# Another split of SBUF homes, earlier unpacking, earlier state sums and two more identity products in a linear-attention and GeGLU kernel

## The chip, the cores and the metric

The kernel runs on one core of a Trainium2 chip. The metric is the device time of one execution in microseconds; where several runs were made, their median.

## What is computed

The input x is 4 sequences of 512 tokens by 512 channels, in float32. Two residual layers follow each other:

```python
x = x + _L0_attn_ref(_layernorm(x, axis=-1), ...)
x = x + _L0_ffn_ref(_layernorm(x, axis=-1), ...)
```

The first is a gated linear attention with 4 heads of 128, in chunks of 128 tokens (4 chunks per sequence). q, k and v are linear in the normalized x; k is normalized per head; alpha is a sigmoid and beta a softplus of two small linear maps. Within a chunk, scores q k^T are weighted with beta and with a causal decay from the running sum of log(alpha), and multiply v. Across chunks a 128 x 128 state per head is carried: a chunk's result takes q times the state before it, and

```python
new_state = state * td_i + d_i      # d_i = v^T (k * beta * decay to the chunk's end)
```

The second is a GeGLU network with 4096 hidden units. Its three weight matrices come as 4-bit codes with a scale per 32 inputs and are unpacked on the chip:

```python
gelu = jnp.tanh(0.7978845608028654 * (gate + 0.044715 * gate ** 3)) * gate * 0.5 + gate * 0.5
inter = gelu * up
out = jnp.einsum('tn,hn->th', inter, Wd)
```

## The kernel before

All instructions stand in an order written out by hand; each engine runs its own in that order, and semaphores make it wait for others.

**Attention.** For each sequence b there are 12 steps: four products for v (`product_v`, psum tiles pva and pvb), four for q (pq) and four for k (pk, added to its bias by VectorE at L428). A step has a number p, and `behind(p)` issues what goes behind its product. Chunk work runs some steps behind: for each chunk, at p % 3 = 0, the transposed k (tpk, kT) and the decay weights dm (pc, exponentials on ScalarE, a mask on GpSimd, and from chunk 1 on q times the decay, qc, on GpSimd); at p % 3 = 1, the scores sp, multiplied into dm by VectorE (L606); at p % 3 = 2, `chunk_sums`: the state's addition dp (L617), the chunk's result yp (L626, L628), and behind them VectorE's addition of yp to the residual tile xr (L637), whose result SP stores to accd (L638), the state's update on VectorE (L646, L651 or, for the last sequence, four operations at L655), and the second layer norm (`second_norm`). That norm's tile is transposed one step later (tp_f) and split in three parts g (L366 on ScalarE, L367 and L368 on VectorE), which SP stores to DRAM (h, L370).

**MLP.** A product of float32 values is made of three parts of 12 bits each ("hi", "lo", "mi"), so each weight block has three rounded tiles. The 32 gate/up blocks are worked on in 35 rounds, four blocks at a time for one sequence of 512 tokens per round, the sequences in turn. A round holds 12 x tiles, loaded from h (L300). For each block, `gate_up` makes two products (pa with 8 matrix instructions, pb with 4, L777); ScalarE and VectorE make the result t of them (L782, L783), a gelu (L789), the product of gate and up (L794), and its three parts i (L797, L801, L802). `down` multiplies these with the down weights (p_d, L821), adds the sums to four tiles acc (L829, L833) and SP stores these (L836). A product of 512 columns by a 128 x 128 weight is one matrix instruction here. The first MLP rounds (one, two and three blocks) run between the chunk steps of the last sequence: round 0 between its k products, round 1 and 2 with its last chunks.

**Unpacking.** A block of weights is unpacked in six steps: fields (L179), masked (L184), scaled (L188), hi (ScalarE, L194), lo (L197) and mi (L200). `unpack(slots, upto)` issues the next step where it is called: behind two of three attention steps from the second sequence on, and behind MLP products. `more` takes the next fetched block when three large homes are free, and `fetch` issues the six transfers of a gate/up block or the two of a down block.

**Homes.** SBUF is kept in two lists of homes: large ones ([P, 2, T], 4 KB per partition) for weights, q and the transposed x, and small ones ([P, T], 2 KB) for all else. `get` takes the home that has been free longest; `put` gives it back at once when the last reader has been issued, so that the next owner's first writer waits, by semaphores, for those readers and for a DMA that still reads the home. Where no small home is free, half of a large one is taken. PSUM has eight banks for tiles of one kind, which go round in the same way.

**Start.** Eight products of the identity (tile busy, L930) keep TensorE at work until the first normalized tile is there.

Of the kernel before, what the change touches and what calls it, by code (L numbers as in the profile page):

```python
# [14 lines left out]
ALU = mybir.AluOpType  # L15
# [6 lines left out]
P = 128  # L22
# [13 lines left out]
def f32(t):  # L36
    return t.bitcast(F32)
# [3 lines left out]
def tile_gated_linear_attention__then__nvfp4_geglu(  # L41
# [19 lines left out]
    nc = tc.nc  # L61
    B, T, D = x.shape
# [54 lines left out]
                else:  # L117
                    self.free.append(tag)

    two_k = Homes("a", 24, [P, 2, T])  # L120
    one_k = Homes("b", 42, [P, T], two_k)

    def psum(name):
        return fps.tile([P, T], F32, tag="p", name=name)
# [124 lines left out]
    loaded = []  # L249
    queue = []  # L250
    rounding = []

    def fetch():
        if waiting:
# [2 lines left out]

    def more():

        if not loaded or len(two_k.free) < 3:  # L260
            return
        nxt, start = loaded.pop(0)
        fields, masked, scaled, hi, lo, mi = start()

        def third():
            scaled()
            rounding.append(hi)

        def fourth():
            while rounding:  # L270
                rounding.pop(0)()
            lo()
            fetch()

        queue.insert(max(len(queue) - 2, 0), (0, fields))
        queue.extend([(0, masked), (nxt, third), (nxt, fourth), (nxt, mi)])
# [315 lines left out]
    def chunk_scores(b, n):  # L592
        toks = slice(n * P, (n + 1) * P)
        sp = psum(f"sp_{b}_{n}")
        kT = ch.pop("kT")
        for h in range(H):
            nc.tensor.matmul(  # L597
                sp[:, h * P : (h + 1) * P], f32(kT)[:, h * P : (h + 1) * P],
                f32(q_sb[b][h // 2])[:, h % 2, toks], start=True, stop=True,
            )  # L600
        one_k.put(kT)
        one_k.put(k_sb.pop((b, n)))
        if n == NCH - 1:
            two_k.put(*q_sb[b])
        dm = ch["dm"]
        nc.vector.tensor_tensor(f32(dm), sp, f32(dm), ALU.mult)  # L606

    def chunk_sums(b, n):
        v = v_sb.pop((b, n))
        old = state.get(b)  # L610
        if n + 1 < NCH:

            kw, new = ch.pop("kw"), ch.pop("new")
            dp = psum(f"dp_{b}_{n}")
            for h in range(H):
                hs = slice(h * P, (h + 1) * P)
                nc.tensor.matmul(dp[:, hs], f32(kw)[:, hs], f32(v)[:, hs], start=True, stop=True)  # L617
            state[b] = new
            one_k.put(kw)
        one_k.put(v)  # L620
        dm, vb = ch.pop("dm"), ch.pop("vb")
        qc = ch.pop("qc", None)
        yp = psum(f"yp_{b}_{n}")
        for h in range(H):
            hs = slice(h * P, (h + 1) * P)
            nc.tensor.matmul(yp[:, hs], f32(dm)[:, hs], f32(vb)[:, hs], start=True, stop=(n == 0))  # L626
            if n > 0:
                nc.tensor.matmul(yp[:, hs], f32(qc)[:, hs], f32(old)[:, hs], start=False, stop=True)  # L628
        one_k.put(dm, vb)
        if n > 0:  # L630
            one_k.put(qc)
            if b < B - 1 or n + 1 == NCH:
                one_k.put(old)
        a = acc.pop((b, n))

        def sums():
            nc.vector.tensor_tensor(f32(a), f32(a), yp, ALU.add)  # L637
            nc.sync.dma_start(accd[b * NCH + n], f32(a))  # L638

        def rest():  # L640
            if n + 1 < NCH:
                chunk_values(b, n + 1)
            if b < B - 1:
                second_norm(b, n, a)
            if n == 0:
                nc.vector.tensor_copy(f32(new), dp)  # L646
            elif n + 1 == NCH:
                pass
            elif b < B - 1:
                nc.vector.tensor_tensor(f32(new), f32(new), dp, ALU.add)  # L650
            else:  # L651

                for h in range(H):
                    hs = slice(h * P, (h + 1) * P)
                    nc.vector.scalar_tensor_tensor(  # L655
                        f32(new)[:, hs], f32(old)[:, hs], td[b][:, n * H + h : n * H + h + 1],
                        dp[:, hs], ALU.mult, ALU.add,
                    )
                one_k.put(old)
            if b == B - 1:  # L660
                second_norm(b, n, a)

        return sums, rest

# [252 lines left out]
    with tc.manual_schedule():  # L917
        wab_sb = const.tile([P, KC, 2 * H], F32, tag="wab", name="wab_sb")
        bq_sb = const.tile([P, H], F32, tag="bq", name="bq_sb")
        bab_sb = const.tile([P, 2 * H], F32, tag="bab", name="bab_sb")  # L920
        bv_sb, bk_sb = one_k.get("bv"), one_k.get("bk")
        wva = [two_k.get(f"wva{c}") for c in range(KC // 2)]
        wvb = two_k.get("wvb")
        wvb_ = f32(wvb).rearrange("p two (k n) -> p (two k) n", n=VB + 2 * H)
        wq, wk = ([two_k.get(f"w{nm}{c}") for c in range(KC // 2)] for nm in "qk")
        x0 = [load(tile_of(n), f"x0_{n}") for n in range(2)]

        busy = psum("busy")
        for i in range(8):
            nc.tensor.matmul(busy[:, :P], ident, ident, start=True, stop=True)  # L930

        warm = small.tile([P, 1], F32, tag="warm", name="warm")
        nc.scalar.activation(warm, eps_la, AF.Exp)
        for c in range(KC // 2):
            nc.sync.dma_start(f32(wva[c])[:, :, :VA], rows(Wv, c)[:, :, :VA])
        nc.sync.dma_start(
            wab_sb.rearrange("p (c two) n -> p c two n", two=2),
            Wab.rearrange("(c p two) n -> p c two n", p=P, two=2),
        )
        nc.sync.dma_start(f32(bv_sb), bv.partition_broadcast(P))  # L940
        for c in range(KC // 2):
            nc.sync.dma_start(wvb_[:, 2 * c : 2 * c + 2, :VB], rows(Wv, c)[:, :, VA:])
        nc.sync.dma_start(bab_sb, bab.partition_broadcast(P))
        x0 += [load(tile_of(n), f"x0_{n}") for n in range(2, NCH)]
        nc.sync.dma_start(bq_sb, bqT)
        for w, src in ((wq, Wq), (wk, Wk)):
            for c in range(KC // 2):
                nc.sync.dma_start(f32(w[c]), rows(src, c))
        nc.sync.dma_start(f32(bk_sb), bk.partition_broadcast(P))
        for n in range(NCH):  # L950
            xs[1, n] = load(tile_of(NCH + n), f"x1_{n}")

        def first(n):
            first_norm(0, n, x0[n])
            settle()

        for n in range(2):
            first_norm(0, n, x0[n])
        settle()
        nc.gpsimd.tensor_copy(wvb_[:, :, VB:], wab_sb)  # L960
        constants()
        turn("a", 1)
        blocks = mlp()
        p = 0
        for b in range(B):
            for j in range(3 * NCH):
                later = None
                if j < NCH:
                    if b == 0:

                        def between():
                            turn("a", 1)
                            if j + 2 < NCH:
                                first(j + 2)

                        product_v(b, j, between if j + 1 < NCH else None)
                    else:
                        product_v(b, j)
                elif j < 2 * NCH:
                    product_q(b, j - NCH)  # L980
                else:
                    later = product_k(b, j - 2 * NCH)
                if b == B - 1:
                    if j == NCH - 1:
                        two_k.put(*wva, wvb)
                        one_k.put(bv_sb)
                    elif j == 2 * NCH - 1:
                        two_k.put(*wq)
                    elif j == 3 * NCH - 1:
                        two_k.put(*wk)  # L990
                        one_k.put(bk_sb)
                if j == 3 * NCH - 1:
                    two_k.put(*hT[b])
                behind(p)
                if later:
                    later()
                if p in (5, 7):
                    fetch()
                if p > 3 * NCH and p % 3:
                    unpack(1, MT)  # L1000
                p += 1
                if b == B - 1 and j == 2 * NCH - 3:
                    load_x(0, jk)
                if b == B - 1 and j == 2 * NCH + 1:
                    for _ in range(2):
                        next(blocks)
                        behind(p)
                        p += 1
        for _ in blocks:
            behind(p)  # L1010
            p += 1


# [46 lines left out]
```

## Time and profile before

| | |
|---|---|
| median of 3 runs | 1312.18 us (1310.87 to 1312.48) |
| profiled execution, its own time | 1310.72 us |
| its span, first to last instruction | 1309.0 us |
| TensorE busy | 1298.8 us, 99% |
| VectorE busy | 955.3 us, 73% |
| ScalarE busy | 459.5 us, 35% |
| GpSimd busy | 122.6 us, 9% |
| DMA | 236.58 MB, mean 181 GB/s |

Times in the profile are those of one execution. Rows of TensorE are overlapped: one starts before the one ahead of it has left the array, so the time of a run of equal instructions is read from start to start. "Idle before" is the time in which an engine had nothing to run, and the releaser is the instruction whose semaphore ended it. SPq is the queue in which SP issues transfers in order.

### The profile page before, as it was taken

To read this page: it belongs to the slowest core of one execution; us is meant where nothing else is said; L and a number is where in the kernel's file an instruction comes from. 1 tells how busy PE (TensorE), PEld (TensorE's weight loads), DVE (VectorE), ACT (ScalarE), POOL (GpSimd) and SP (SyncE) were. 2 spreads that over 40 slices of the span, in tenths; PEclk is the share of its full clock that TensorE was granted. 3 is DMA by queue.
4 is the path that set the end of the run, shared out by engine and by line. 5 is a ranking of instruction groups with operands and counts; after the bars stand their busy time and mean duration, and the time that the engine had idled before them with its cause. 6 is when DMAs were issued, how large, how long until landed. Compare 5 with 4: busy or idle time off the path is not lost.

```text
span 1309.0 us, 17051 instructions
## 1 busy us (share of the span) xinstructions
PE 1298.8 (99%) x5822; PEld 1042.1 (80%) x5822; DVE 955.3 (73%) x1523; ACT 459.5 (35%) x906; POOL 122.6 (9%) x215
## 2 busy tenths in 40 slices
PE   9999999999999999999999999999999999999998
PEld 6677676778888888888888888888888888887886
DVE  3466666788767777777777777777777777777566
ACT  1443334753333333333333333333333333332332
POOL 1546363510000000000000000000000000000000
PEclk9999999999999999999999999999999999999999
DMA  7034436788555565656555555555555555555463
GB/s 242 9 97 132 120 104 201 237 263 276 189 174 196 176 195 176 193 175 195 181 190 182 189 183 187 184 187 183 187 185 186 180 190 186 184 178 194 167 247 132
DMA packets 173943, 236.58 MB, mean 181 GB/s; under 512 B 15776, under 2 KB 74400, under 8 KB 173856
## 3 DMA queue, kind: packets, MB, share of 16 engines
q1 hardware_dynamic: 173856, 235.49, 55.5%
q8 instruction: 46, 0.75, 0.2%
q14 instruction: 41, 0.34, 0.1%
HBM read 183.00 MB, written 52.43 MB: 180 GB/s over the span
## 4 chain that ended last, share of the span: by engine, by line
PE 96%; DMA 2%; DVE 1%; ACT 0%; issue 0%; POOL 0%; SPq 0%; DVEq 0%; ACTq 0%; POOLq 0%
PE pa L777 35%; PE p_d L821 26%; PE pb L777 17%; PE pk L422 4%; PE pq L410 4%; PE pva L385 2%; PE pvb L392 2%; DMA x<-h 1%; PE sp L597 1%; PE yp L626 1%; PE yp L628 1%; PE dp L617 1%; PE tp_a L345 1%; PE tp_f L345 1%; PE tpk L530 0%; PE pc L540 0%
## 5 line engine op out<-in xcount | busy, mean ns | idle before, releaser
L777 PE MATMUL pa<-x,wgu 128*128 128x512 f32 x2048 | 506.7, 389 | 0.0
L777 PEld LDWEIGHTS pa<-x,wgu 128*128 128x128 f32 x2048 | 383.9, 188 | 79.5
L821 PE MATMUL p_d<-wd,i 128*128 128x512 f32 x1542 | 356.5, 389 | 2.2 <-DVE state L655 1.1
L821 PEld LDWEIGHTS p_d<-wd,i 128*128 128x128 f32 x1542 | 288.3, 188 | 64.8 <-DVE i L801 1.6
L782 ACT ACTIVATE t<-pb 128x512 f32<-128x512 f32 x256 | 151.3, 591 | 359.8 <-PE pb L777 356.5
L777 PE MATMUL pb<-x,wgu 128*128 128x512 f32 x1024 | 274.8, 389 | 0.8 <-DMA x<-h 0.5
L783 DVE TENSOR_TENSOR t<-pa,t 128x512 f32<-128x512 f32 x256 | 176.5, 689 | 83.5 <-ACT t L782 78.1
L777 PEld LDWEIGHTS pb<-x,wgu 128*128 128x128 f32 x1024 | 192.2, 188 | 42.1 <-DMA x<-h 2.3
L829 DVE SCALAR_TENSOR_TENSOR acc<-p_d,acc 128x512 f32<-128x512 f32 (+1 forms) x137 | 93.3, 682 | 124.0 <-PE p_d L821 124.0
L797 ACT ACTIVATE i<-t 128x512 fp32r<-128x512 f32 x128 | 81.1, 633 | 192.4 <-DVE t L794 189.4
L789 ACT ACTIVATE t<-t 128x512 f32<-128x512 f32 x128 | 81.1, 633 | 135.5 <-DVE t L783 135.4
L801 DVE TENSOR_TENSOR i<-t,i 128x512 fp32r<-128x512 f32 x128 | 88.7, 693 | 23.6 <-ACT i L797 21.8
L833 DVE TENSOR_TENSOR acc<-acc,p_d 128x512 f32<-128x512 f32 x135 | 92.9, 688 | 14.1
L852 POOL TENSOR_TENSOR acc<-acc,last 128x512 f32<-128x512 f32 x1 | 1.3, 1289 | 1015.0 <-ACT last L851 1015.0
L794 DVE SCALAR_TENSOR_TENSOR t<-t,t 128x512 f32<-128x512 f32 x128 | 88.6, 692 | 4.3
L802 DVE SCALAR_TENSOR_TENSOR i<-i,t 128x512 fp32r<-128x512 f32 x128 | 88.1, 689 | 0.0
L422 PE MATMUL pk<-wk,hT 128*128 128x512 f32 x128 | 57.4, 592 | 0.0
L410 PE MATMUL pq<-hT,wq 128*128 128x512 f32 x128 | 57.4, 592 | 0.0
L410 PEld LDWEIGHTS pq<-hT,wq 128*128 128x128 f32 x128 | 23.7, 190 | 23.7 <-issue 23.2
L422 PEld LDWEIGHTS pk<-wk,hT 128*128 128x128 f32 x128 | 23.5, 190 | 23.6 <-issue 23.4
L200 DVE TENSOR_TENSOR wgu<-wgu,wgu 128x1024 fp32r<-128x1024 f32 x32 | 39.0, 1218 | 0.0
L197 DVE SCALAR_TENSOR_TENSOR wgu<-wgu,w_gu 128x1024 fp32r<-128x1024 f32 x32 | 38.9, 1216 | 0.0
(127 smaller groups left out, 941.5 us busy)
## 6 DMA issues: line engine op xcount, KB each, us to landing
x<-h SPq DMA_DIRECT2D x420, 256.0 KB
acc<-acc SPq DMA_DIRECT2D x256, 256.0 KB
h<-g SPq DMA_DIRECT2D x48, 256.0 KB
x<-in_x SPq DMA_DIRECT2D x16, 256.0 KB
pk_gu<-in_gate_p SPq DMA_DIRECT2D x32, 128.0 KB
sc_gu<-in_gate_s SPq DMA_DIRECT2D x64, 64.0 KB
pk_gu<-in_up_p SPq DMA_DIRECT2D x32, 128.0 KB
sc_gu<-in_up_s SPq DMA_DIRECT2D x64, 64.0 KB
```

The source lines that it names most:

```text
L410: nc.tensor.matmul(pq, f32(wq[k // 2])[:, k % 2, h * P : (h + 1) * P], f32(hT[b][k // 2])[:, k % 2, :], start=(k == 0), stop=(k == KC - 1),)
L422: nc.tensor.matmul(pk, f32(hT[b][k // 2])[:, k % 2, n * P : (n + 1) * P], f32(wk[k // 2])[:, k % 2, :], start=(k == 0), stop=(k == KC - 1),)
L777: nc.tensor.matmul(o, w3[j][:, k % 2, c * P : (c + 1) * P], x[j * KC + k], start=(j == js[0] and k == 0), stop=(j == js[-1] and k == KC - 1),)
L782: nc.scalar.activation(f32(t), pb, AF.Copy, scale=-1.0 / ONE_E)
L783: nc.vector.tensor_tensor(f32(t), pa, f32(t), ALU.add)
L789: nc.scalar.activation(f32(g), f32(g), AF.Gelu_apprx_tanh, scale=ONE_E)
L794: nc.vector.scalar_tensor_tensor(f32(u), f32(g), ONE_E, f32(u), ALU.mult, ALU.mult)
L801: nc.vector.tensor_tensor(il, f32(u), f32(ih), ALU.subtract)
L802: nc.vector.scalar_tensor_tensor(im, f32(ih), ONE_E, f32(u), ALU.mult, ALU.subtract)
L821: nc.tensor.matmul(banks[key_][:, part], inter[i][j][:, n * P : (n + 1) * P], wd[ms[i] // 2][j][:, ms[i] % 2, part], start=(i == 0 and j i ...
L829: nc.vector.scalar_tensor_tensor(a, banks[n, False, part.start][:, part], ONE_E, a, ALU.mult, ALU.add)
L833: nc.vector.tensor_tensor(a, a, banks[n, True, 0], ALU.subtract)
```

## The change

The homes are split anew: 28 large and 34 small ones instead of 24 and 42 (each large one is as big as two small ones, so the sum is the same). `more` keeps two large homes back (`kept`), except at some steps of the last but one sequence and once the chunk steps are done. From the second sequence's products for k on, `unpack` is called behind each attention step, not only behind two of three. For the last sequence, the state's products dp and its update on VectorE are issued with the chunk's scores, ahead of the step's transposes and of the MLP product beside them, and not behind the chunk's results; the other sequences keep theirs. Ten identity products are issued at the start instead of eight.

```diff
-    two_k = Homes("a", 24, [P, 2, T])
-    one_k = Homes("b", 42, [P, T], two_k)
+    two_k = Homes("a", 28, [P, 2, T])
+    one_k = Homes("b", 34, [P, T], two_k)
...
+    kept = [2]
...
-        if not loaded or len(two_k.free) < 3:
+        if not loaded or len(two_k.free) < 3 + kept[0]:
...
+        if b == B - 1:
+            add = state_sums(b, n)
         dm = ch["dm"]
         nc.vector.tensor_tensor(f32(dm), sp, f32(dm), ALU.mult)
+        if b == B - 1:
+            add()
+
+    def state_sums(b, n):
+
+        v = v_sb[b, n]
+        old = ch["old"] = state.get(b)
+        if n + 1 == NCH:
+            return lambda: None
+        kw, new = ch.pop("kw"), ch.pop("new")
+        dp = psum(f"dp_{b}_{n}")
+        for h in range(H):
+            hs = slice(h * P, (h + 1) * P)
+            nc.tensor.matmul(dp[:, hs], f32(kw)[:, hs], f32(v)[:, hs], start=True, stop=True)
+        state[b] = new
+        one_k.put(kw)
+
+        def add():
+            if n == 0:
+                nc.vector.tensor_copy(f32(new), dp)
+            elif b < B - 1:
+                nc.vector.tensor_tensor(f32(new), f32(new), dp, ALU.add)
+            else:
+
+                for h in range(H):
+                    hs = slice(h * P, (h + 1) * P)
+                    nc.vector.scalar_tensor_tensor(
+                        f32(new)[:, hs], f32(old)[:, hs], td[b][:, n * H + h : n * H + h + 1],
+                        dp[:, hs], ALU.mult, ALU.add,
+                    )
+
+        return add
 
     def chunk_sums(b, n):
...
+        add = state_sums(b, n) if b < B - 1 else None
+        old = ch.pop("old")
+        one_k.put(v_sb.pop((b, n)))
...
-            one_k.put(qc)
-            if b < B - 1 or n + 1 == NCH:
-                one_k.put(old)
+            one_k.put(qc, old)
...
+            second_norm(b, n, a)
+            if add:
+                add()
...
-        for i in range(8):
+        for i in range(10):
             nc.tensor.matmul(busy[:, :P], ident, ident, start=True, stop=True)
...
+                kept[0] = 0 if b == B - 2 and NCH <= j < 3 * NCH - 2 else 2
...
-                if p > 3 * NCH and p % 3:
+                if p > 3 * NCH and (p % 3 or p > 5 * NCH):
                     unpack(1, MT)
...
+            if not chunk_of(p):
+                kept[0] = 0
```

More of the change, by code (lines that the diff above doesn't have):

```diff
@@ L604, in chunk_scores @@
             two_k.put(*q_sb[b])
+        if b == B - 1:
+            add = state_sums(b, n)
         dm = ch["dm"]
         nc.vector.tensor_tensor(f32(dm), sp, f32(dm), ALU.mult)
-    def chunk_sums(b, n):
[L609 to L620, printed above, removed]
+        if b == B - 1:
[25 more added lines that the diff above has]
+        return add
+    def chunk_sums(b, n):
+        add = state_sums(b, n) if b < B - 1 else None
+        old = ch.pop("old")
+        one_k.put(v_sb.pop((b, n)))
         dm, vb = ch.pop("dm"), ch.pop("vb")
@@ L642, in rest @@
                 chunk_values(b, n + 1)
[L643 to L661, printed above, removed]
+            second_norm(b, n, a)
+            if add:
+                add()
         return sums, rest
```

## The prediction

> **What bounds the kernel.** The page comes first, for the engine that is always busy.
>
> ```profile
> PE 1298.8 (99%) x5822; PEld 1042.1 (80%) x5822; DVE 955.3 (73%) x1523; ACT 459.5 (35%) x906; POOL 122.6 (9%) x215
> PE 96%; DMA 2%; DVE 1%; ACT 0%; issue 0%; POOL 0%; SPq 0%; DVEq 0%; ACTq 0%; POOLq 0%
> ```
>
> TensorE is busy 99% of 1309.0 us and carries 96% of the chain that ended last. No product is added or removed except two on the identity, so the time can move only where TensorE idles, or where it will idle after the change. The windows view (columns: busy us of PE, PEld, DVE, ACT, POOL, then clock, DMA share, GB/s) tells where:
>
> ```profile
> 120.00:180.00 60.00, 60.00 (x296) 42.40 (x295) 40.78 (x87) 25.46 (x81) 31.75 (x52) 1.00 0.38 114
> 180.00:228.00 48.00, 48.00 (x233) 34.39 (x232) 28.35 (x68) 16.66 (x45) 17.52 (x30) 1.00 0.53 165
> 260.00:296.00 36.00, 33.66 (x174) 27.47 (x173) 32.51 (x53) 18.15 (x31) 6.04 (x9) 1.00 0.83 272
> 296.00:328.60 32.60, 32.60 (x146) 26.99 (x145) 27.36 (x42) 12.48 (x21) 0.00 (x0) 1.00 0.81 266
> ```
>
> From 120 to 228 TensorE never idles. It does between 228 and 296, where the last sequence's chunks run between the first MLP rounds, and in the first 11 us. The timeline of TensorE shows both (start, length, then in brackets the idle time before and its releaser):
>
> ```profile
> 1.52 3.79 PE L930 MATMUL busy<-ident 128*128 128x128 f32 x16 [1.52 <-POOL ident masks.py:199]
> 6.01 1.12 PE L345 MATMUL tp_a<-ident,hn_a 128*128 128x128 f32 x4 [0.70 <-DVE hn_a L324]
> 7.59 3.79 PE L385 MATMUL pva<-wva,hT 128*128 128x264 f32 x8 [0.46 <-ACT hT L355]
> ...
> 264.17 0.46 PE L626 MATMUL yp<-vb,dm 128*128 128x128 f32 x2 [0.59 <-DVE dm L606]
> ...
> 265.94 2.77 PE L821 MATMUL p_d<-wd,i 128*128 128x512 f32 x11
> 269.87 3.24 PE L821 MATMUL p_d<-wd,i 128*128 128x512 f32 x13 [1.15 <-DVE state L655]
> ...
> 276.83 1.14 PE L777 MATMUL pb<-x,wgu 128*128 128x512 f32 x2 [0.36 <-DMA x<-h]
> ```
>
> An MLP product takes 0.227 us (eight in 1.81 in the chain). By that, four places lose: the last pb of round 1 (246.27 to 249.56, 3.29 for 2.72: 0.57), yp of chunk 2 (dp at 262.52 takes 0.89, yp starts at 264.17: 0.76), round 1's down products (265.94 to 272.95, 7.01 for 24 x 0.227 = 5.44: 1.57), round 2's x (273.62 to 277.81, 4.19 for 2.72: 1.47). Together 4.4 us, which is all that can be had here.
>
> Last the queue of SP (SPq) and the chain's DMA rows, for how long a transfer takes:
>
> ```profile
> 237.48 6.55 SPq L300 DMA_DIRECT2D x<-h  x12
> 244.35 0.32 SPq L638 DMA_DIRECT2D acc<-xr  x1
> ...
> 262.93 2.67 SPq L370 DMA_DIRECT2D h<-g  x3
> ```
>
> ```profile
> 248.50 3.19 DMA h<-g
> 257.51 6.65 DMA x<-h
> ```
>
> SP issues one transfer per 0.54 us. A store with little before it landed 3.19 us after its issue, a load behind five others 6.65.
>
> **Identity products.** One takes 3.79/8 = 0.47 us, so ten end at 6.26 instead of 5.31. The first transposes start at 6.01 now: 0.25 later. Against this stands the clock. The clock column reads 1.00 here too, but the eight pva records from 7.59 take 3.62 to the next row, and the same eight from 13.38 take 1.78: half speed until about 11.2, 3.6 us into the work that starts at 7.59. The identity products alone, 3.79 us in one piece, did not release it; with ten of them TensorE works in one piece from 1.52 to 7.38. If that brings full speed by 7.6, 1.84 - 0.25 = 1.6 us are gained; if not, 0.25 is lost. The rows do not decide it; I take -0.7, near the middle, and keep both ends. [...]
>
> **Unpacking.** The instruction order of both kernels shows that by the first MLP round VectorE has done eight more large steps (w_d, wd_1, wd_2, fields and mask of a gate-up block, w_gu, wgu_1, wgu_2), ScalarE two roundings (L194). At 1.27 + 1.22 + 1.22 + 0.76 + 0.69 + 3 x 1.22 by their rows (L188, L197, L200, L179, L184) that is 8.8 us off VectorE after 228, spread over 120 to 228, where it is busy 69.1 of 108: 77.9 after. A step is at most 1.2 us ahead of a row that TensorE waits for, and PE's 108 us there have no idle time that shows the slack; I take 0, and 1.2 for each place where the cover fails, three at most. ScalarE loses 2 x 1.05 after 228. The six transfers of a weight fetch leave SP's queue at 250.00 to 253.94, ahead of x loads; they and a down fetch now stand before earlier h stores, where DMA is at 0.38: nothing. Keeping two homes back does not delay a step in that order. From round 3 on the order is the same.
>
> **State sums.** dp (0.89) moves ahead of the step's transposes and pa; state's four operations (1.1) ahead of g. The 1.15 wait on state goes. The next bank that the down products need is the one that ScalarE's second t of round 1 empties, then VectorE's t, then yp's.
>
> **Homes.** Here the change pays. Thirty-four small homes instead of 42 are reused sooner, and the order names new waits, which hold up an engine in order. Chunk 3's k (L428) now gets the home of chunk 0's xr, so VectorE waits for the store at 244.35 above. Round 2's second x load gets a home that VectorE reads at round 1's i (L802) first, and SP stands there with five loads, three h stores, four acc loads and six loads behind it. Round 1's last t (L782, ScalarE) gets the home of the g that was just made, so it waits for an h store behind those loads. Round 2's first t waits for the last acc store of round 1. None of these is in the old kernel. On its time axis:
>
> First, k. g and its stores come 0.6 later (the state copy is ahead of them), so the store is issued at 244.95. Its landing lies between 3.2 and 6.65 later; it stands behind twelve loads, near the upper end: 5.5, so 250.45. k 0.69 and dm 0.6 on VectorE: 251.75. TensorE, with dp done, wants yp at 246.27 + 0.89 + 2.72 = 249.9: 1.9 lost (0 to 3.0). The x wait of 0.57 is covered by dp's 0.89. Behind k on VectorE wait dm, state, g and t, behind squares of k on ScalarE t and gelu.
>
> Second, the down products. yp of chunk 2 loses 0.25 instead of 0.76 and starts at 264.95, down at 266.7. VectorE's i of the step before ends near 263.5 (262.8 now), which frees SP; five issues later, at 266.2, the h store goes out. It lands 3.2 to 6.65 later, five loads before it: 4.5, so 270.7. ScalarE's t 0.6: 271.3. TensorE wants that bank at the ninth product, 268.5: 2.8 lost. Then it follows VectorE: t 0.69 (0.5 lost), t and xr (0.85), two i (0.73): 4.9 lost in all, for 1.57 now, so +3.3 (1.1 to 5.5).
>
> Third, x of round 2: SP and TensorE are both about 4 us later. I keep 1.47: 0 (-1.5 to +1.5). Fourth, yp of chunk 3: acc's eight adds end near 281.0, the store lands by 284.4, t, t and dm take 1.9: 286.3, where TensorE wants yp at about 285.5: +0.8 (0 to 2).
>
> In steady rounds five x loads now wait for homes that the round's last product (at 322.25 in the round from 303.21 to 335.85, so 19.0 us into 32.6) reads first. By 22 they are out and by 29 landed, needed at 32.6: 0.
>
> **Sum.** +1.9 - 0.57 - 0.51 + 3.3 + 0.8 = +4.9, and -0.7 for the clock: +4.2. The profiled execution took 1310.72 (span 1309.0): 1314.9. The runs' median, 1312.18, is 1.46 above that execution; I suspect the clock's arrival in the start, which the ten products would even out, so I add nothing. Against the median it is +2.7, just over 0.2% (2.6 us), which is about what a measurement of this kernel can tell from no change.
>
> **Rivals.** The clock comes early in most executions and the two stores land near their lower ends: -1.6 and about +4, 1313.1, no difference to be told. For it: the idle 0.70 that is filled. Against: the stores stand behind loads. Chance 0.34.
>
> Faster: the h store of round 1's g goes out before the blocked loads matter, because VectorE, rid of 8.8 us, ends that i before 259; then t is not late, and the waits on dm and state are gone. That decides: with i at 259 the store lands by 266.3 and TensorE's ninth product waits for nothing. Then -0.57 - 0.51 - 1.57 + 0.5 for k, -1.6 for the clock: 1307.0. Against: i needs ScalarE's rounding behind exp, gelu and two table loads of 1.28. Chance 0.06.
>
> Much slower: SP's blocked loads become the bound, round 2's x lands 3 us late and the cover of unpacking fails in two places: 1314.9 + 3 + 2.4, capped by overlap near 1319. Chance 0.10. The forecast has 0.50; by itself it runs from 1313.5 to 1316.8, and a sixth of it is within the bound.
>
> Slower by over 0.2%: 0.42 + 0.10 = 0.52; within: 0.08 + 0.34 = 0.42; faster 0.06. The range leaves out the faster rival and the far end of the slow one: 1312.2 to 1317.8.
>
> **What would show it.** In the profile after: k L428's last row with idle of 4 us or more and a store as releaser; ScalarE's t L782 with idle near 8 us before the down products; SPq idle ahead of round 2's second x load; no wait on state; 120 to 228 still full; pva's first eight in 1.9 or 3.8 us. If TensorE runs through the down products of round 1 without idle time, the forecast is wrong; if 120 to 228 shows gaps, so is the cover.

## The result

The changed kernel takes 1316.94 us (median of 6 runs, 1316.35 to 1318.82), the kernel before 1311.21 (6 runs beside it): ratio 1.0047, 95% interval 1.0034 to 1.0060. It is slower, by over 0.2%, as forecast; the time is 2.0 above the forecast one (1314.9) and inside the range (1312.2 to 1317.8), though 0.1 above the stretch that the forecast by itself was given (1313.5 to 1316.8). The profiled execution took 1316.35, its span 1314.6, against 1310.72 and 1309.0.

### The profile page after: what moved, and what is told of

Read it like the earlier page. It is cut to its first block, busy times and chain, and to the rows that moved or that the text cites. A ratio compares the mean times of both kernels' runs of the same rounds, so it can differ in the third digit from the quotient of the medians.

```text
span 1314.6 us, 16984 instructions
## 1 busy us (share of the span) xinstructions
PE 1300.5 (99%) x5826; PEld 1041.9 (79%) x5826; DVE 954.1 (73%) x1523; ACT 459.4 (35%) x906; POOL 124.8 (9%) x215
## 4 chain that ended last, share of the span: by engine, by line
PE 94%; DMA 2%; DVE 2%; issue 1%; SPq 1%; ACT 1%; POOL 0%; DVEq 0%; ACTq 0%; POOLq 0%
PE pa L785 34%; PE p_d L829 26%; PE pb L785 17%; PE pq L411 4%; PE pk L423 4%; PE pvb L393 2%; PE pva L386 2%; PE yp L652 1%; PE sp L598 1%; PE yp L654 1%; PE dp L623 1%; PE tp_a L346 0%; PE tpk L531 0%; PE tp_f L346 0%; DMA h<-g 0%
## 5 line engine op out<-in xcount | busy, mean ns | idle before, releaser
L188 DVE SCALAR_TENSOR_TENSOR w_gu<-i_gu,sc_gu 128x1024 f32<-128x1024 f16 x32 | 39.5, 1233 | 0.0
```

## The profile after

Lines that answer to those shown of before. The page first:

```profile
PE 1300.5 (99%) x5826; PEld 1041.9 (79%) x5826; DVE 954.1 (73%) x1523; ACT 459.4 (35%) x906; POOL 124.8 (9%) x215
PE 94%; DMA 2%; DVE 2%; issue 1%; SPq 1%; ACT 1%; POOL 0%; DVEq 0%; ACTq 0%; POOLq 0%
```

TensorE carries 94% of the last chain instead of 96%. The windows (same columns as before):

```profile
120.00:180.00 60.00, 60.00 (x296) 42.38 (x295) 44.20 (x93) 25.57 (x82) 35.31 (x51) 1.00 0.39 115
180.00:228.00 48.00, 48.00 (x235) 34.25 (x234) 31.76 (x69) 18.13 (x45) 18.24 (x29) 1.00 0.56 178
260.00:296.00 36.00, 31.62 (x154) 24.46 (x153) 22.98 (x40) 15.82 (x28) 5.64 (x10) 0.91 0.72 241
296.00:328.60 32.60, 32.60 (x145) 27.01 (x144) 26.21 (x40) 10.96 (x18) 0.00 (x0) 1.00 0.75 250
271.00:278.00 7.00, 6.52 (x15) 4.11 (x16) 6.27 (x11) 2.13 (x6) 0.81 (x2) 0.54 0.82 279
```

120 to 228 is still full, with VectorE busy 76.0 there instead of 69.1 (77.9 forecast); so are the steady rounds. From 260 to 296 TensorE idles 4.4 us instead of 2.3, and the clock column, 1.00 everywhere before, reads 0.91: the last line shows 0.54 from 271 to 278. TensorE's timeline:

```profile
1.52 3.86 PE L938 MATMUL busy<-ident 128*128 128x128 f32 x20 [1.52 <-POOL ident masks.py:199]
7.20 2.05 PE L386 MATMUL pva<-wva,hT 128*128 128x264 f32 x8 [0.46 <-ACT hT L356]
250.77 0.49 PE L652 MATMUL yp<-vb,dm 128*128 128x128 f32 x2 [1.60 <-DVE dm L609]
265.87 2.09 PE L829 MATMUL p_d<-wd,i 128*128 128x512 f32 x8
271.38 7.25 PE L829 MATMUL p_d<-wd,i 128*128 128x512 f32 x16 [3.41 <-ACT t L790]
280.97 1.35 PE L785 MATMUL pb<-x,wgu 128*128 128x512 f32 x4
287.19 0.46 PE L652 MATMUL yp<-vb,dm 128*128 128x128 f32 x2 [0.78 <-DVE dm L609]
```

The start is better: pva's first eight in 2.05 instead of 3.79. Two new stops stand in front of yp of chunk 1 and in front of the ninth down product of round 1, which waits for ScalarE's t. Who held VectorE and ScalarE, each from its own timeline:

```profile
249.42 0.69 DVE L429 TENSOR_TENSOR k<-pk,bk 128x512 f32<-128x512 f32 x1 [7.92 <-DMA acc<-xr]
```

```profile
270.73 0.60 ACT L790 ACTIVATE t<-pb 128x512 f32<-128x512 f32 x1 [6.71 <-DMA h<-g]
285.12 0.60 ACT L790 ACTIVATE t<-pb 128x512 f32<-128x512 f32 x1 [2.44 <-DMA acc<-acc]
```

Three stores are waited for, since the next owner of a home may not write before the store has read it. The prediction's signs are there: k idle by 4 us or more (7.92), t by about 8 (6.71). SP's queue:

```profile
259.09 5.95 SPq L301 DMA_DIRECT2D x<-h  x6
265.14 1.62 SPq L371 DMA_DIRECT2D h<-g  x3
266.86 1.19 SPq L301 DMA_DIRECT2D xr<-in_x  x1
271.42 2.04 SPq L301 DMA_DIRECT2D acc<-acc  x4
273.55 2.75 SPq L301 DMA_DIRECT2D x<-h  x6
```

Six loads take 5.95 where six take 2.75 further down: the second stands from 259.4 to 262.8. Then SP stands from 268.0 to 271.4 at the acc loads, so the last six x loads of round 2 begin at 273.55 instead of 268.61. The chain that ended last ties it together (start, length, what):

```profile
244.06 5.24 DMA acc<-xr
249.42 0.06 DVE k L429
...
262.06 0.70 DVE i L810
262.82 0.32 SPq L301
...
265.14 5.47 DMA h<-g
270.73 0.61 ACT t L790
```

xr's store holds k; what follows k on VectorE and GpSimd ends in the i that frees SP's blocked load; behind SP's loads comes the store of g, and it holds t.

## Experiments: which part costs the time

Each ratio is to runs of the kernel before on the same chip (medians of 1309.9 to 1310.3). Differences between two experiments are those of their medians; as the two did not always run on the same chip, the figure by the ratios stands beside where it differs.

**The homes alone** (with `kept`, which is in this run too), in the kernel before:

```diff
-    two_k = Homes("a", 24, [P, 2, T])
-    one_k = Homes("b", 42, [P, T], two_k)
+    two_k = Homes("a", 28, [P, 2, T])
+    one_k = Homes("b", 34, [P, T], two_k)
...
+    kept = [2]
```

> The kernel before with 28 large and 34 small homes and with kept; unpacking, state sums and the eight products as they were. Theory A: the order names the same wait of chunk 3's k for the store of chunk 0's xr, and ScalarE's last t of round 1 waits for the second h store of the g just made: 1315 to 1320, with yp of chunk 1 and round 1's down products late. Rival B: 1310 to 1313, since homes alone move nothing that TensorE waits for.

Measured: 1323.8 (1320.14 to 1324.47), ratio 1.0101 (1.0087 to 1.0115). More than A's range: the homes and `kept` together cost 13.9 us, over twice what the whole change does. Every run with 34 homes has `kept`, so its share is not known. ScalarE's timeline has the named wait, 3.5 us later than in the changed kernel:

```profile
274.20 0.60 ACT L783 ACTIVATE t<-pb 128x512 f32<-128x512 f32 x1 [7.32 <-DMA h<-g]
```

**The changed kernel with the old split**:

```diff
-    two_k = Homes("a", 28, [P, 2, T])
-    one_k = Homes("b", 34, [P, T], two_k)
+    two_k = Homes("a", 24, [P, 2, T])
+    one_k = Homes("b", 42, [P, T], two_k)
```

> The changed kernel with the old split of homes (24 large, 42 small); kept, the earlier unpacking, the early state sums and the ten products stay. With fewer large homes some unpacking steps come later again. Theory A (the smaller number of small homes costs the time: VectorE's k behind the store of xr, SP's loads and ScalarE's t behind the stores of g): no wait of these is left, so the 2.2 us lost at round 1's x and yp and the 7.2 us at round 1's down products go back to at most what the kernel before lost there, 0.6 and 1.6; the median is 1310 to 1312.5, at or below the kernel before (1311.2). Rival B (the state sums put in front of the step, or the unpacking, cost the time): the split changes little, 1315 or more.

Measured: 1310.52, ratio 1.0005 (0.9996 to 1.0014). A's range holds and B is out, though the time is not below that of the kernel before (1309.88 beside it), only not told from it. Unpacking steps move with the number of large homes, so this run alone does not separate the two; the next one, where earlier unpacking is a gain, does.

**The changed kernel with unpacking at its old places**:

```diff
-                if p > 3 * NCH and (p % 3 or p > 5 * NCH):
+                if p > 3 * NCH and p % 3:
```

> The changed kernel with the old places of unpacking (behind two of three steps), everything else as changed. The homes alone made 1323.8, the whole change 1316.9, so the other parts give back about 7 us under 34 homes. Theory A: most of this is unpacking (8.8 us of VectorE's and 2.1 of ScalarE's work no longer stands between the blocked steps after 228): 1320 to 1324, with round 1's i later and SP's blocked loads later with it. Rival E: it is the early state sums (the wait of the down products on state): 1316 to 1318.

Measured: 1321.9, ratio 1.0091 (1.0077 to 1.0104). A holds: under 34 homes the earlier unpacking is worth 5.0 us (5.8 by the ratios). VectorE's timeline of this run shows how:

```profile
257.04 1.21 DVE L197 SCALAR_TENSOR_TENSOR wd<-wd,w_d 128x1024 fp32r<-128x1024 f32 x1
261.88 1.22 DVE L200 TENSOR_TENSOR wd<-wd,wd 128x1024 fp32r<-128x1024 f32 x1
266.05 0.69 DVE L810 SCALAR_TENSOR_TENSOR i<-i,t 128x512 fp32r<-128x512 f32 x1 [1.32 <-POOL qc L560]
```

Large steps stand between the blocked ones again, and the i that frees SP starts at 266.05 instead of 262.06.

**The changed kernel with the state sums at their old place** (`state_sums` undone):

> The changed kernel with the state sums at their old place (behind the chunk's results) also for the last sequence; 28 and 34 homes, kept, earlier unpacking and ten products stay. Theory A (the loss comes from the homes and the early state sums give little under it): the down products again wait for state, but behind the same stores: 1316.5 to 1318. Rival G (the early state sums delay g, its stores and so SP by the 1.1 us of state's four operations): 1315 to 1316. Rival H (they are what gives back most after unpacking): 1319 or more.

Measured: 1318.29, ratio 1.0061 (1.0049 to 1.0074); A, at the upper end of its range. By the medians the early state sums give 1.4 us under 34 homes, but this interval and the changed kernel's (1.0034 to 1.0060) overlap, so the gain is not shown. The wait on state is back behind that on t:

```profile
275.89 5.91 PE L822 MATMUL p_d<-wd,i 128*128 128x512 f32 x13 [1.20 <-DVE state L656]
```

## Experiments: which wait

The next four keep every engine's order of the changed kernel and only hand out homes differently; the last of them has one small home more.

**k on another home**:

```diff
-            tag = self.free.pop(0)
+            tag = self.free.pop(-1 if name == "k_3_3" else 0)
```

> The changed kernel, with one home exchanged: chunk 3's k takes the home of the last sq (read by nothing, written by ScalarE before) instead of chunk 0's xr, whose store VectorE waits for; every engine's order is that of the changed kernel. Theory A: VectorE's idle 7.9 us ahead of k shrinks by some 5, yp of chunk 1 no longer idles 1.6 us; 0.7 stay for x of round 1; all behind it comes 1.6 to 2.1 us earlier, g's stores and x loads too: median 1314.8 to 1315.4 against 1316.9. Rival C (SP's blocked queue in round 1 and 2 sets the end whatever k does): less than 0.5 us gained.

Measured: 1316.2, ratio 1.0047 (1.0034 to 1.0059), the same ratio as the changed kernel's. In the profile k came 4.2 us earlier (VectorE's timeline) and yp of chunk 1 did not wait, but t still waited for its store (TensorE's timeline):

```profile
245.18 0.69 DVE L429 TENSOR_TENSOR k<-pk,bk 128x512 f32<-128x512 f32 x1 [3.00 <-ACT sq L437]
```

```profile
270.58 7.29 PE L829 MATMUL p_d<-wd,i 128*128 128x512 f32 x16 [3.20 <-ACT t L790]
```

Between 232 and 251 the profiled execution won 1.8 us on the changed kernel's; at its end 1.3 were left (0.6 of span, beside a start 0.7 later), after a wait of 0.7 for ScalarE's t at yp of chunk 2 that the changed kernel does not have. The medians show 0.7, the ratios nothing. A's 1.6 to 2.1 did not come through, and the times do not settle whether C's 0.5 is passed.

**t on another home**:

```diff
-            tag = self.free.pop(0)
+            tag = self.free.pop({'xr15': 1}.get(name, 0))
```

> The changed kernel with two homes exchanged: chunk 15's xr load takes the home of g's first part, and ScalarE's last t of round 1 the free home that xr had; every engine's order is that of the changed kernel. Theory A (two paths end together): t no longer waits, round 1's down products lose 1 to 2 us instead of 7.2 and the clock stays full there; but SP still stands at the acc loads until g's stores have landed (271.4), so the last x load of round 2 lands near 281.8 as before and TensorE waits 4 to 6 us there instead: total -0.5 to +1.0, 1316.4 to 1318. Rival D (the prediction's own step: t's wait is the price of round 1): 3 to 5.5 us gained, 1311.5 to 1314.

Measured: 1316.6, ratio 1.0047 (1.0033 to 1.0061). D is out: the stop in the down products went, and nothing was won. TensorE's timeline and SP's:

```profile
266.25 6.26 PE L829 MATMUL p_d<-wd,i 128*128 128x512 f32 x24
274.95 0.66 PE L531 MATMUL tpk<-ident,k 128*128 128x128 f32 x4 [2.44 <-DVE acc L837]
276.34 3.68 PE L785 MATMUL pa<-x,wgu 128*128 128x512 f32 x8
```

```profile
270.65 0.35 SPq L301 DMA_DIRECT2D xr<-in_x  x1
271.37 2.04 SPq L301 DMA_DIRECT2D acc<-acc  x4
```

A is right on the time but not on the place: it had TensorE wait 4 to 6 us at x of round 2, where the wait was 0.35. SP's acc loads wait for g's stores as before, so VectorE's first addition to acc is late and TensorE stands 2.44 for it; after that it runs at about half speed, eight products of pa in 3.68 instead of 2.00.

**Three waits out** (k, t, and the acc and x loads on homes of round 1's x tiles):

> The changed kernel with k of chunk 3 on sq's home, xr 15 and the last t of round 1 exchanged, and SP's acc loads of round 1 and the last six x loads of round 2 on homes of round 1's x tiles, which TensorE has read, instead of on homes of g that still are stored; every engine's order, the number of homes and all other parts are those of the changed kernel. Theory A (these reuses are the whole loss): x of round 2 is issued 4 to 5 us earlier, nothing but the gelu and i chain holds round 1's down products: 4 to 6 us below the changed kernel, 1311 to 1313. Rival B (the loss lies in the order, in unpacking or state sums at other places): 1314.5 or more.

Measured: 1315.67, ratio 1.0041 (1.0029 to 1.0054). A's range failed, and B's number held, but not for B's reason. ScalarE's timeline:

```profile
270.62 0.63 ACT L805 ACTIVATE i<-t 128x512 fp32r<-128x512 f32 x1 [6.97 <-DMA h<-g]
```

The homes of g that t and the loads had left went to the next in line, round 1's i, which waited for the same stores.

**All waits out**:

```diff
+    stored = [f"g{j}_3_1" for j in range(3)]
+    soon = ["t1_1_1", "x_2_1_2", "x_2_1_3", "x_2_2_0"] + [f"acc_1_{t}" for t in range(4, 8)] + [f"i{j}_1_1" for j in range(3)]
+    late = ["x_2_2_1", "x_2_2_2", "x_2_2_3"]
...
+            if name in late:
+                at = min(i for i, t in enumerate(self.free) if t in self.hot)
+            elif name in soon:
+                at = min(i for i, t in enumerate(self.free) if t not in self.hot)
+            elif name == "k_3_3":
+                at = -1
+            tag = self.free.pop(at)
+            if name == "xr15":
+                self.free.insert(0, tag)
+                tag = "b34"
...
+            if name in stored:
+                self.hot.append(tag)
```

> The changed kernel, every engine's order as changed. In the run with three waits out a fourth took their place: ScalarE's i of round 1's last block (L805) had got a home of g and stood 7 us for its store. Here none of the owners that come next has a home of that g: k of chunk 3 is on sq's home, the last t of round 1 on the free one, the acc loads, three x loads and the i of round 1 on homes of round 1's x tiles, the last three x loads of round 2 on g's homes, and xr 15 alone on a 35th small home. Theory A (home reuse after g is the whole loss, wherever it falls): ScalarE's i starts before 268, round 1's down products lose 1 to 2 us, the last x load of round 2 is issued by 272 and lands by 278 instead of 281.8: 1311.5 to 1313.5. Rival F (the loads land when the DMA engines are through with what is queued, whoever waits at SP): x of round 2 lands at 280 or later all the same, 1314 to 1316.

Measured: 1313.0 (1312.02 to 1313.59), ratio 1.0019 (1.0010 to 1.0028). A's range holds, F is out: TensorE was through with x of round 2 at 277.97. Only the down products lost more than A said, 2.6 instead of 1 to 2. ScalarE's, TensorE's and SP's timelines:

```profile
266.05 0.63 ACT L823 ACTIVATE i<-t 128x512 fp32r<-128x512 f32 x1 [3.04 <-DVE t L820]
```

```profile
264.39 6.22 PE L847 MATMUL p_d<-wd,i 128*128 128x512 f32 x24
272.41 0.66 PE L549 MATMUL tpk<-ident,k 128*128 128x128 f32 x4 [1.80 <-DVE acc L855]
273.80 3.36 PE L803 MATMUL pa<-x,wgu 128*128 128x512 f32 x8
```

```profile
269.23 3.37 SPq L319 DMA_DIRECT2D x<-h  x6
```

The 24 down products run in one piece, and the x loads begin 4.3 us earlier than in the changed kernel. With every order kept, better owners for a few homes, one of them the 35th, win 3.9 us (3.7 by the ratios); what the 35th home alone is worth was not measured. Still left over the kernel before are 2.7; of these the 1.80 for acc's loads and the stretch at half clock behind it (0.76 from 271 to 278, pa in 3.36) can be seen.

## Experiments: the clock, and 42 homes

**Filling the stop** in front of the ninth down product:

```diff
+                        if key == "1" and n == 2:
+                            for _ in range(6):
+                                sums(n, [i], (0, 1), again=True)
                         sums(n, [i])
```

> The changed kernel; in round 1's down products the two products ahead of the 3.4 us stop (hi and lo of the third token tile) are made seven times instead of once, 12 extra products, 2.7 us, inside the stop; the result is the same. Theory A (TensorE's clock was halved from 270.6 to 277.4 because TensorE stood still for 3.4 us): the clock stays at 1.00 and the products from 274 on take 0.23 instead of 0.43 us, so the down products end 1.5 to 2 us earlier; but the last x load of round 2 landed at 281.8 and was needed at 281.8, and its issue hangs on SP and the g stores, not on TensorE, so the time comes back there: total 0 to -0.5 us, 1316.4 to 1316.9, with x of round 2 waiting 1.5 to 2 us. Rival B: the half clock is the price itself and nothing waits behind it: 1315 to 1315.4. Rival C: the clock halves all the same (something other than idle time lowers it): no change and half-speed rows in 271 to 278.

Measured: 1317.5, ratio 1.0060 (1.0048 to 1.0073). B is out. A did not get what it asked for: waits of 0.55, 0.23 and 0.59 remained between the products, and the clock halved later and for less long (from 274.1 to 277.5, in the changed kernel from 270.7 to 277.5). This execution also ran at half clock from 250.2 to 253.6, before the place of the edit, which the changed kernel's did not; so its time is no clean comparison. This run does not separate A from C. A window ahead of the edit (clock 1.00 in the changed kernel), and the same window as above:

```profile
245.00:252.50 7.50, 5.65 (x23) 4.26 (x23) 3.61 (x9) 3.47 (x11) 2.54 (x6) 0.85 0.52 180
271.00:278.00 7.00, 5.63 (x15) 3.38 (x15) 5.76 (x10) 2.40 (x6) 0.80 (x2) 0.76 0.82 260
```

**Ten products alone**, in the kernel before:

> The kernel before with ten identity products instead of eight, nothing else. In the four profiles with ten products the clock was full by 4.4 to 7.1 us and the first eight pva records took 2.05 us; in the two with eight it came at 10.1 and 11.2. [...] That gives 1.2 to 2.2 us in somewhat over half of the executions and -0.3 in the others: median 0.6 to 1.3 below the kernel before, slowest run nearer to the median. Rival B: the first norms set the start in any case, two products more only move it: 0 to +0.3.

Measured: 1309.36 (1307.43 to 1309.85, 11 runs) against 1310.18 (1308.50 to 1311.36): ratio 0.9992 (0.9983 to 1.0001). The size, 0.8, is inside the expected 0.6 to 1.3, but the interval just reaches 1, so the gain is likely and not shown. The slowest run is 0.5 above the median, where the kernel before has 1.2, as expected. In how many executions the gain comes was the author's estimate; no run shows it. pva's first eight take 2.05 in all twelve profiles with ten products, 3.79 and 3.21 in the two with eight:

```profile
7.45 2.05 PE L385 MATMUL pva<-wva,hT 128*128 128x264 f32 x8 [0.46 <-ACT hT L355]
```

**Ten products and early state sums** at 24 and 42:

> The kernel before (24 and 42 homes, unpacking as before) with the early state sums and ten identity products. The prediction took 1.15 us off the down products' wait on state and 0.5 off yp of chunk 2. Theory A (what is won there is lost at x of round 2, whose loads SP issues no earlier): 1309.5 to 1311, not below ten products alone (1309.4). Rival J: the two gains hold: 1307.5 to 1308.5.

Measured: 1311.33 (1308.55 to 1312.18), ratio 1.0005 (0.9996 to 1.0014). J is out, and the time is 0.3 above A's range too: with 42 homes the early state sums win nothing over ten products alone, and rather lose, though the two intervals just overlap. In the profiled execution A's reason is seen. The transposed k behind the down products starts at 270.18, with ten products alone at 271.29; but x of round 2 holds both, and the scores behind it start together (this run, then ten products alone):

```profile
276.75 1.05 PE L598 MATMUL sp<-q,kT 128*128 128x128 f32 x8
276.76 1.05 PE L597 MATMUL sp<-q,kT 128*128 128x128 f32 x8
```

The 11 runs fall into two groups, four from 1308.55 to 1309.61 and seven from 1311.18 to 1312.18. The profiled one (1309.59) is of the faster, so what the slower lose stays open.

**Ten products and earlier unpacking**, 24 and 43 homes, state sums as before:

> The parts without their price: the kernel before with kept, the earlier unpacking and the ten products, the state sums at their old place, 24 large homes and 43 small ones (one more than before; it fits). Theory A (the homes were the loss; ten products give 0.8; earlier unpacking takes VectorE's work out of the blocked stretch): round 1's down products wait 0.7 less, 1308 to 1309.5, below the kernel before by 1 to 2. Rival B (unpacking in 120 to 228 costs TensorE time there): at or above 1310.

Measured: 1309.04 (1308.31 to 1309.57), ratio 0.9992 (0.9983 to 1.0001). A's range holds; B is out. It is the fastest median here, 1.3 below the kernel before, but not surely told from it, nor from ten products alone. The down products wait 0.76 for state instead of 1.15, which is 0.4 less, where A had 0.7:

```profile
268.50 3.29 PE L822 MATMUL p_d<-wd,i 128*128 128x512 f32 x13 [0.76 <-DVE state L656]
```

## Why the prediction was right, and where its sizes were not

The mechanism was the one forecast: 34 small homes are reused sooner, and VectorE's k, ScalarE's t, SP's loads and the next round's t wait for stores. Step by step, in the two profiled executions:

| step | predicted | measured | from |
|---|---|---|---|
| clock and start | -0.7 | -1.78 | the sums of log(alpha) (cps, L500, before L499) at 33.74 for 35.52 |
| x of round 1 | -0.57 | +0.09 | 0.66 lost at its pb |
| k, yp of chunk 1 | +1.9 | +2.11 | the next pa at 252.57 for 252.15, less the two above |
| yp of chunk 2 | -0.51 | -0.49 | down products at 265.87 for 265.94 |
| round 1's down products | +3.3 | +5.58 | 265.87 to 278.46: 12.59 for 7.01 |
| x of round 2 | 0 | -1.17 | 0.30 lost there instead of 1.47 |
| yp of chunk 3 | +0.8 | +1.04 | the next pa at 288.97 for 283.59, less the above; 0.95 of it ahead of yp |
| rest | 0 | +0.20 | |
| sum | +4.2 | +5.58 | span 1314.6 for 1309.0 |

**Luck**: the sum (1.4 off) came nearer than its terms. The misses were +2.3 at round 1's down products and +0.7 at x of round 1, against -1.2 at x of round 2 and -1.1 in the start. And against the medians the change is +5.7, twice the +2.7 that the prediction gave: its three runs of the kernel before (1312.18) lay above the six here (1311.21) and the 27 of the last experiments (1310.33).

**Held**: xr's landing (5.24 after issue, 5.5 assumed), t's start (270.73, 270.7 worked out, though by two errors that cancel: g's store went out at 265.14 and not 266.2, and took 5.47 and not 4.5), yp of chunk 2, yp of chunk 3, no wait on state, 120 to 228 full, the steady rounds, and that SP stands ahead of round 2's second x load.

**Round 1's down products** were mis-sized, 5.6 for 3.3. The stop came at 267.8 instead of 268.5, since TensorE was ahead by the faster start while t was not: 3.6 lost instead of 2.8. And the sum ran all products at full speed, where eight, from 274.02 to 277.52, took 3.50 us instead of 1.81: 1.7 that no term had. The window from 271 to 278, clock 0.54, shows it. The clock was halved inside the wait of 3.41, at 270.7, and full again at 277.5; that the wait brought it on is the author's reading, and the prediction had reckoned with the clock in the start only.

**x of round 2** took part of that back: it was put at 0, and TensorE came 5.5 us later, SP 4.9. The run with t's home exchanged shows the same from the other side: t's wait and SP's wait end nearly together, so to remove one wins nothing. The prediction added them as terms in a row; what it said of x there was a bound, and the bound (-1.5) held it.

**x of round 1** failed as a term. dp in front was to cover 0.57; but SP's last load there went out only 0.30 earlier while TensorE came 0.9 earlier, dp included, so the same wait came back.

**Unpacking** was taken as 0. That TensorE loses nothing to it at 120 to 228 is right. That it gives 5.0 us back after 228 stood in no term: the terms of the homes were worked out on the new order and had it inside. So the parts were not priced apart. By one comparison of medians each: homes with `kept` +13.9, earlier unpacking -5.0, early state sums -1.4 and ten products -0.8, the last two within the noise. They need not add up to the whole (5.7), since each was measured with other parts beside it. The early state sums show it: under 42 or 43 homes the two runs with ten products that leave them out stand at 0.9992, and the two that have them at 1.0005.

**The clock**: -0.7 was near the middle, ten products alone measured -0.8 in the medians; the two profiles differ by 1.8 because the one of before came up late (11.2) and the one of after early (4.4).

## What to carry to other kernels

Before homes or buffers are cut, list for each that is freed by a store who takes it next and what stands behind that owner on its engine; other owners for a handful of homes, and one home more, were worth 3.9 us here with no instruction moved. Before a wait is credited as a gain, ask what else ends at the same moment: the removal of one of two equal waits measured nothing, and the try with three waits out only handed the home to the next owner. Price an idle stretch of TensorE with the slow stretch after it, not by its length alone: behind the 3.41 us in the changed kernel eight products took 1.7 more, and behind the 1.80 with all waits out pa took 3.36 instead of 2.00.

## What was not expected of the hardware

The clock fell at some waits of TensorE and not at others. It reads 1.00 from 245 to 284 in the kernel before, where the longest wait there is 1.15. From 271 to 278 it reads 0.54 in the changed kernel (a wait of 3.41), 0.51 with three waits out (3.26) and 0.76 with all waits out (1.80). But the length of a wait does not settle it: in front of yp of chunk 1 the changed kernel waits 1.60, and the clock stays at 1.00 from 245.0 to 252.5 with pairs of yp 0.22 apart; with the stop filled the same place waits 1.56, and the clock reads 0.85 there with the pairs 0.43 apart. These are single executions, and no two profiles here are of one kernel; what decides it no run shows.

In the start the executions differ too. In the profile of the changed kernel the clock was full at 4.4, while the ten identity products ran (1.52 to 5.38); in that of the kernel before, the eight ended without it (1.52 to 5.31), and it came at about 11.2. Why it came so early in the one is not shown.
